# Reordering the attention head stage of a two-layer cross-attention kernel: third four's scores ahead of a projection, second four's sums ahead of the third scores by keys, one copy moved to ScalarE

## The chip, the cores and the metric

The kernel runs on one core of one Trainium2 chip. The metric is the device time in microseconds (us) of one execution. Of the kernel before there are three runs, 228.4, 233.35 and 229.08 us; their median is 229.08 us. One more execution was profiled; every duration and time of day below comes from it. Engines are named as the profile names them: PE (TensorE), PEld (its weight loads), DVE (VectorE), ACT (ScalarE), POOL (GpSimd), SP (the queue that issues most loads).

## The reference, cut to what matters

Inputs are `x` and `ctx`, both 32 x 256 x 256 in float32. Layer 0 (L0) is an attention of 16 heads of 16 columns, of which only the result for batch 0 is used: it is added to every batch. Layer 1 (L1) normalises both sides, attends over 256 keys, goes through a hidden layer of 4, and attends once more on itself.

```python
def _L0_xattn_ref(tgt, memory, Wq, Wk, Wv):
    ...
    scores = jnp.einsum('bhqd,bhkd->bhqk', q, k) * scale
    probs = jax.nn.softmax(scores, axis=-1)
    att = jnp.einsum('bhqk,bhkd->bhqd', probs, v)
    ...
    tgt2 = att[0]
    return tgt + tgt2
x = _L0_xattn_ref(x, ctx_1024, ...)
x = _L1_xattn_ref(ctx_1024, x, ...)
```

So nothing of L1 that depends on `x` can begin before L0's `att` for batch 0 is there. What depends on `ctx` alone (its normalised rows) can be made during L0.

## The kernel before, in words

The order of the work is written out by hand: the program's calls are recorded in the order of the source, each engine has its own queue and takes its instructions in that order, and waits between engines are put in where data or buffers need them.

L0 (lines 670 to 736) works on batch 0. The 16 heads go in four groups of four, `j` = 0 to 3, called fours here. For each four:

- `head_queries(j)` (L477): eight matmuls give the scores by queries, `sq`, four banks of PSUM with two halves each (L445).
- `head_maxima(j, sq, heads)` (L484): one DVE reduction per head, the negated row maximum, into `m_all` (L486). Its second argument allows a part of the heads.
- `head_less(j)` (L490): PE turns the maxima (`pm`, L493); the function it returns has DVE add them to the queries, `qmT` (L498).
- `head_keys(j)` (L500): eight matmuls give the scores by keys, `sk`, with the maxima already taken off; ACT takes the exponential of each head into `eT_h` (L507).
- `head_values(j, copy)` (L512): eight matmuls give the weighted sums and the denominators, `ph` (L357); `copy` brings them to SBUF as `col_h` (L368). The copy is ACT's unless `by_vector` (DVE) is given.
- `head_turned(j)` (L522): PE turns the sums (`pt_h`, L375); the function it returns has DVE divide (a reciprocal `rd_h`, L527, and a product into `att`, L528).

The banks for `sq` and `sk` are taken in turn from six (`four_banks`, L456), so a new group of scores waits for the maxima or exponentials of an older one. `pm`, `ph`, `pt_h`, the projection of the values (`project_values`, L427, matmul L430, copied by ACT into `v1`, L437) and the small bias product (`setup_bias`, L576: matmuls `p_b1f` L579, then the DVE sum `fc1b_all` L582) share two banks under the tag "tp".

Between these stand the preparations for L1. `stats(n)` (DVE, L211) takes the statistics of batch `n` of `ctx`, two instructions for each batch. `moments_c(q)` (POOL, L222 to L236) makes from four such batches the factors `rs_c` and `nmr_c`; it needs the statistics of all four. `even_normed` (POOL, L316) normalises even rows and `odd_normed` (ACT, L322) odd rows with these factors. `moments_ahead(2)` (L269) does part of this on DVE and has POOL compute a power (`rs_c`, L227).

L0 ends with the products for fours 2 and 3 into `att`. Then `add_attention` has POOL issue a DMA that adds `att` to four batches of `x` (L751), and `add_first` (L827) has DVE add `att` to batch 0 itself (L828) and take its statistics, after which POOL computes its `rs_x` (L227). These are followed by the steps of L1: normalised rows, scores, softmax, sums, and then the second half of L1.

Of the kernel before, what the change touches and what calls it, by code (L numbers as in the profile page):

```python
# [22 lines left out]
QB = 4  # L23
# [4 lines left out]
def tile_xattn_seq(  # L28
# [51 lines left out]
    def bank(tag, name):  # L80
        return ps.tile([P, NC, D], F32, tag=tag, name=name)
# [131 lines left out]
    def moments(st, n, name, eng=None):  # L213

        eng = eng or nc.gpsimd

        def t(what, c=1, bufs=2):
            return small.tile([P, n, c], F32, tag=f"{what}{n}", name=f"{what}_{name}", bufs=bufs)

        sm, df, sq, v4, ve, nm = t("sm", 2), t("df"), t("sq"), t("v4"), t("ve"), t("nmean")  # L220
        rs, nmr = t("rs", 1, 3), t("nmr", 1, 3)
        eng.tensor_sub(df, st[:, :, 1:2], st[:, :, 4:5])  # L222
        eng.tensor_add(sm, st[:, :, 1:3], st[:, :, 4:6])
        eng.tensor_mul(sq, df, df)
        eng.tensor_scalar(v4, sm[:, :, 1:2], 4.0 / D, 4 * EPS, ALU.mult, ALU.add)
        eng.tensor_add(ve, v4, sq)
        nc.gpsimd.tensor_tensor(  # L227
            rs.rearrange("p n o -> p (n o)"),
            ve.rearrange("p n o -> p (n o)"),
            neg_half[:, 0:n],  # L230
            ALU.pow,
        )

        def product():
            eng.tensor_scalar(nm, sm[:, :, 0:1], -0.5, 0.0, ALU.mult, ALU.add)
            eng.tensor_mul(nmr, nm, rs)  # L236

        if eng is nc.gpsimd:
            product()
            return rs, nmr  # L240
        return rs, nmr, product
# [11 lines left out]
    def stats_c(n):  # L253
        q, b = n // QB, n % QB
        statistics(st_tile(q - 1)[:, 0, b], cq_of[q][:, b])
# [5 lines left out]
    def flat(st):  # L261
        return st.rearrange("p b t c -> p (b t) c")

    def moments_c(q):
        rn = moments(flat(st_of[q - 1][:, 0]), TQ, f"c{q}")
        for b in range(QB):
            mc_of[q * QB + b] = *rn, b * NC
# [44 lines left out]
    def even_normed(*ns):  # L312
        for n in ns:
            rs, nmr, i = mc_of[n]
            row = cq_of[n // QB][:, n % QB, 0, :]
            nc.gpsimd.tensor_scalar(row, row, rs[:, i, :], nmr[:, i, :], ALU.mult, ALU.add)  # L316

    def odd_normed(*ns):
        for n in ns:
            rs, nmr, i = mc_of[n]  # L320
            row = cq_of[n // QB][:, n % QB, 1, :]
            nc.scalar.activation(  # L322
                row, row, AF.Identity, bias=nmr[:, i + 1, :], scale=rs[:, i + 1, :]
            )
# [22 lines left out]
    def by_columns(psum, name, weights, moving, copy=nc.vector.tensor_copy, by_pairs=False):  # L347
        return copy_columns(columns(psum, name, weights, moving, by_pairs), name, copy)
# [22 lines left out]
    def tokens_first(psum, src, name):  # L371

        pt = psum(f"pt_{name}")
        for t in range(NC):
            nc.tensor.transpose(pt[:, 0, t * P : (t + 1) * P], src[:, t * P : (t + 1) * P], ident)  # L375
        return pt[:, 0, :].rearrange("p (t b c) -> p t b c", t=NC, c=SL)
# [50 lines left out]
    def project_values(t, copy):  # L427
        pp = bank("tp", f"pp_v{t}")
        for dc in range(NC):
            nc.tensor.matmul(  # L430
                pp[:, t, :],
                c0T[:, dc, t * P : (t + 1) * P],
                wvT[:, dc, :],
                start=(dc == 0),
                stop=(dc == NC - 1),
            )
        copy(v1[:, t, :, 0:DK], pp[:, t, :].rearrange("p (h e) -> p h e", e=DK))  # L437

    def pair_products(*pairs):

        for t in range(NC):
            for p, lhs, rhs, dst in pairs:
                for i in range(2):
                    r = SL * (p % 2 * 2 + i)
                    nc.tensor.matmul(  # L445
                        dst[i][:, t, :],
                        lhs[r : r + SL, t * P : (t + 1) * P],
                        rhs[r : r + SL, :],
                        start=True,
                        stop=True,  # L450
                    )
# [4 lines left out]
    def four_banks(name):  # L456

        at = head_banks[0]
        head_banks[0] = (at + QB) % 6
        return [  # L460
            ps0.tile([P, NC, D], F32, tag=f"h{i}", name=f"{name}_{i}")
            if i < QB
            else bank("et", f"{name}_{i}")
            for i in ((at + n) % 6 for n in range(QB))
        ]
# [8 lines left out]
    def head_of(j, i):  # L474
        return 8 * (j // 2) + 2 * i + j % 2

    def head_queries(j):  # L477

        sq = four_banks(f"sq{j}")
        qk = qT[:, j, :], kT[:, j, :]  # L480
        pair_products((0, *qk, sq[0:2]), (1, *qk, sq[2:4]))
        return sq

    def head_maxima(j, sq, heads):  # L484
        for i in heads:
            nc.vector.tensor_reduce(  # L486
                m_all[:, j % 2, :, i, ones_at[j % 2]], sq[i], AX.X, ALU.max, negate=True
            )

    def head_less(j):  # L490
        pm = bank("tp", f"pm_{j}")
        for t in range(NC):
            nc.tensor.transpose(  # L493
                pm[:, 0, t * P : (t + 1) * P],
                m_all[:, j % 2, t].rearrange("p b c -> p (b c)"),
                ident,
            )
        return lambda: nc.vector.tensor_add(qmT[:, j % 2, :], pm[:, 0, :], qT[:, j, :])  # L498

    def head_keys(j):  # L500

        sk = four_banks(f"sk{j}")
        kq = kT[:, j, :], qmT[:, j % 2, :]
        pair_products((0, *kq, sk[0:2]), (1, *kq, sk[2:4]))
        eT_of[j] = wk.tile([P, QB, NC, D], F32, tag="eTq", name=f"eT_h{j}", bufs=2)
        for i in range(QB):
            nc.scalar.activation(eT_of[j][:, i], sk[i], AF.Exp)  # L507
# [4 lines left out]
    def head_values(j, copy=nc.scalar.copy, by_pairs=False):  # L512
        col_of[j] = by_columns(
            tp_bank,
            f"h{j}",
            lambda kt, i: v1[:, kt, head_of(j, i), :],
            eT_of.pop(j),
            copy,
            by_pairs,
        )  # L520

    def head_turned(j):  # L522
        pa = tokens_first(tp_bank, col_of.pop(j), f"h{j}")

        def weighted():
            rd = small.tile([P, NC, QB, 1], F32, tag="rdh", name=f"rd_h{j}")
            nc.vector.reciprocal(rd, pa[:, :, :, DK : DK + 1])  # L527
            nc.vector.tensor_mul(  # L528
                att.rearrange("p t (k i e d) -> p t k i e d", i=QB, e=2, d=DK)[
                    :, :, j // 2, :, j % 2, :  # L530
                ],
                pa[:, :, :, 0:DK],
                rd.to_broadcast([P, NC, QB, DK]),
            )

        return weighted
# [39 lines left out]
    def setup_bias():  # L576
        pb = bank("tp", "p_b1f")
        for dc in range(NC):
            nc.tensor.matmul(  # L579
                pb[:, 0, 0:FH], ones, b1f[:, dc, :], start=(dc == 0), stop=(dc == NC - 1)  # L580
            )
        nc.vector.tensor_add(fc1b_all, pb[:, 0, 0:FH], fc1b_bc)  # L582
# [80 lines left out]
    by_vector = nc.vector.tensor_copy  # L663

    def stats(*ns):
        for n in ns:
            stats_c(n)
# [6 lines left out]
    sq = head_queries(0)  # L674
# [5 lines left out]
    sq = head_queries(1)  # L680
    less = head_less(0)
# [8 lines left out]
    head_less(1)()  # L690
    setup_outer()
    stats(3)
    project_values(1, on_scalar)
    moments_c(0)
    even_normed(0, 1, 2, 3)
    sq = head_queries(2)
    stats(4)
    head_maxima(2, sq, (0, 1))
    head_values(0)
    setup_bias()  # L700
    head_maxima(2, sq, (2, 3))
    head_keys(1)
    odd_normed(0, 1)
    weighted = head_turned(0)
    stats(5)
    head_less(2)()
    weighted()
    sq = head_queries(3)
    stats(6)
    head_maxima(3, sq, range(QB))  # L710
    head_values(1)
    odd_normed(2, 3)
    head_keys(2)
    weighted = head_turned(1)
    stats(7)
    moments_c(1)
    even_normed(4, 5)
    head_less(3)()
    weighted()
    head_keys(3)  # L720
    stats(8, 9, 10)
    head_values(2, by_vector)
    stats(11)
    odd_normed(4)
    head_values(3, on_scalar, True)
# [1 line left out]
    weighted = head_turned(2), head_turned(3)  # L727
# [633 lines left out]
```

## Time and profile before

| what | from | us |
|---|---|---|
| median of three runs | times | 229.08 |
| the profiled execution's own time | times | 233.63 |
| its span | page | 231.9 |
| PE, DVE, ACT, POOL busy over the span | page, part 1 | 214.7, 169.8, 146.8, 174.8 |
| L0's last part, from `qmT` of the second four to the sum into batch 0 | chain | 17.65 to 34.89 |
| DVE busy in 34.90 to 48.60 | busy time by stretch | 12.33 of 13.70 |
| POOL busy in 48.60 to 96.00 | busy time by stretch | 43.67 of 47.40 |
| PE busy in 96.00 to 160.00 | busy time by stretch | 62.81 of 64.00 |

A line of the timeline reads: start, duration, engine, line of the source, operation, output and inputs, shapes, how many instructions were merged, and in brackets the idle time before it with the engine and line that ended it. Durations overlap a little with the next instruction's start, so steps are best taken from start to start. A line of the chain reads start, duration, engine, tile and line. The profiled execution is 4.55 us longer than the median of the runs; the granted clock of PE was 1.00 in every stretch up to 190 us and 0.83 in the stretch from 190.00 to 231.90, far behind the part that is changed.

### The profile page before, as it was taken

How to read it: one execution, taken by the hardware profiler on the slowest of the kernel's cores; microseconds unless marked ns; L12 is line 12 of the kernel's file. 1: busy time of each engine (PE TensorE's matmuls, PEld its weight loads, DVE VectorE, ACT ScalarE, POOL GpSimd, SP SyncE). 2: the span in 40 equal slices, each digit the busy share in tenths (PEclk: the TensorE clock that was granted, in tenths of full speed). 3: DMA queues.
4: the chain of work that ended last, by engine and by line, in shares of the span. 5: the costliest groups of instructions: out<-in, count | busy, mean ns of one | idle time of the engine just before them, and what ended most of it. 6: DMA issues, size and time to landing. Idle time of an engine off the chain costs nothing.

```text
span 231.9 us, 4950 instructions
## 1 busy us (share of the span) xinstructions
PE 214.7 (93%) x1797; PEld 155.8 (67%) x1797; DVE 169.8 (73%) x409; ACT 146.8 (63%) x299; POOL 174.8 (75%) x276
## 2 busy tenths in 40 slices
PE   7999898898999989999999999989989999999960
PEld 6766556576787768697897887866665666566540
DVE  1797989899988748667686686766384866588791
ACT  2544978698988285966789967456846753444410
POOL 6057598576989999999979999995189999993000
PEclk9999999999999999999999999999999995699996
DMA  6789997999959964180720000000000130444477
GB/s 212 271 310 371 394 383 148 194 256 236 207 104 335 275 117 170 34 151 2 133 51 1 3 0 0 3 4 4 4 0 3 51 133 0 181 184 181 185 281 264
DMA packets 18038, 33.81 MB, mean 146 GB/s; under 512 B 1175, under 2 KB 2142, under 8 KB 18014
## 3 DMA queue, kind: packets, MB, share of 16 engines
q1 hardware_dynamic: 12974, 24.33, 29.3%
q0 software_dynamic: 3696, 7.34, 18.1%
q10 hardware_dynamic: 1344, 1.84, 2.3%
q8 instruction: 14, 0.23, 0.4%
q14 instruction: 10, 0.08, 0.1%
HBM read 17.73 MB, written 8.39 MB: 113 GB/s over the span
## 4 chain that ended last, share of the span: by engine, by line
PE 53%; POOL 23%; DVE 14%; ACT 5%; issue 2%; DVEq 0%; POOLq 0%; ACTq 0%
PE sc L779 13%; POOL x_all L770 5%; PE k L445 4%; PE pt_x L202 4%; PE o L445 3%; PE pt_c L202 3%; POOL cq L307 3%; DVE st L211 3%; PE pt_e L202 3%; PE pu L357 3%; POOL rs_b L227 3%; PE sc L445 2%; POOL rs_x L227 2%; PE ph L357 2%; PE pf L357 2%
## 5 line engine op out<-in xcount | busy, mean ns | idle before, releaser
L779 PE MATMUL sc<-nxT,nfT 128*128 128x256 f32 x256 | 62.4, 386 | 0.7 <-ACT nfT L761 0.7
L779 PEld LDWEIGHTS sc<-nxT,nfT 128*128 128x128 f32 x256 | 45.7, 190 | 12.1 <-issue 5.3
L770 POOL TENSOR_TENSOR x_all<-x_all,w_bc 128x512 f32<-128x512 f32 x32 | 39.8, 1273 | 0.0
L792 ACT ACTIVATE e<-sc,nm 128x256 f32<-128x256 f32 x64 | 26.9, 473 | 19.0 <-DVE nm L789 18.8
L789 DVE TENSOR_REDUCE nm<-sc 128x2 f32<-128x512 f32 x32 | 22.0, 688 | 22.9 <-PE sc L779 11.1
L761 ACT ACTIVATE nfT<-pt_x,bq,wq 128x256 f32<-128x256 f32 x64 | 33.3, 583 | 1.6 <-PE pt_x L202 1.5
L1214 DVE TENSOR_TENSOR x_all<-o,x_all 128x512 f32<-128x512 f32 (+1 forms) x22 | 19.4, 927 | 8.0 <-PE o L445 8.0
L211 DVE BATCH_NORM_STATS2 st<-x_all 128x6 f32<-128x256 f32 x64 | 23.2, 411 | 0.6 <-DMA x_all<-att 0.5
L1209 ACT ACTIVATE eT<-k 128x1024 f32<-128x1024 f32 (+1 forms) x16 | 14.2, 916 | 13.2 <-PE k L445 10.5
L202 PE MATMUL pt_x<-ident,x_all 128*128 128x128 f32 x132 | 20.8, 280 | 1.5 <-POOL x_all L329 1.3
L202 PE MATMUL pt_c<-ident,cq 128*128 128x128 f32 x132 | 19.7, 276 | 1.5 <-ACT nfT L761 1.0
L202 PE MATMUL pt_e<-ident,e 128*128 128x128 f32 x128 | 19.5, 275 | 1.3 <-ACT eTq L801 0.7
L211 DVE BATCH_NORM_STATS2 st<-cq 128x6 f32<-128x256 f32 x56 | 20.6, 412 | 0.0
L307 POOL TENSOR_SCALAR cq<-cq,rs_b,nmr_b 128x256 f32<-128x256 f32 x32 | 19.4, 680 | 0.0
L202 PEld LDWEIGHTS pt_e<-ident,e 128*128 128x128 f32 x128 | 15.4, 141 | 5.0 <-ACT e L792 1.6
L202 PEld LDWEIGHTS pt_x<-ident,x_all 128*128 128x128 f32 x132 | 15.5, 143 | 4.7 <-POOL x_all L329 2.4
L801 ACT COPY eTq<-pt_e 128x512 f32<-128x512 f32 x32 | 18.4, 588 | 0.3 <-PE pt_e L202 0.3
L345 DVE COPY nxT<-pt_c 128x512 f32<-128x512 f32 x23 | 15.6, 677 | 2.3 <-PE pt_c L202 2.3
L202 PEld LDWEIGHTS pt_c<-ident,cq 128*128 128x128 f32 x132 | 15.0, 141 | 3.1 <-ACT nfT L761 1.9
L331 ACT ACTIVATE x_all<-x_all,nmr_b,rs_b 128x256 f32<-128x256 f32 x16 | 9.8, 618 | 10.9 <-POOL nmr_b L236 10.9
L445 PE MATMUL o<-w_out,vt 32*128 32x256 f32 x128 | 15.0, 448 | 0.6 <-ACT vt L1088 0.5
L445 PE MATMUL k<-tt,ut 32*128 32x256 f32 x112 | 15.3, 441 | 0.1
(222 smaller groups left out, 443.8 us busy)
## 6 DMA issues: line engine op xcount, KB each, us to landing
out_dram<-x_all SPq DMA_DIRECT2D x16, 512.0 KB
x_all<-att POOLq DMA_DIRECT2D x7, 1024.0 KB, 9.3
cq<-in_ctx_dram SPq DMA_DIRECT2D x6, 1024.0 KB
x_all<-in_x_dram SPq DMA_DIRECT2D x4, 1024.0 KB
x_all<-in_x_dram SPq DMA_DIRECT2D x1, 2048.0 KB
x_all<-in_x_dram SPq DMA_DIRECT2D x1, 1792.0 KB
cq<-in_ctx_dram ACTq DMA_DIRECT2D x1, 1024.0 KB
cq<-in_ctx_dram SPq DMA_DIRECT2D x1, 768.0 KB
```

The lines of the kernel that those rows point to most:

```text
L202: nc.tensor.transpose(pt[:, dc, t * P : (t + 1) * P], src[:, t, dc * P : (dc + 1) * P], ident)
L211: nc.vector.bn_stats(st[:, t, :], src[:, t, :])
L307: nc.gpsimd.tensor_scalar(row, row, rs[:, i + t, :], nmr[:, i + t, :], ALU.mult, ALU.add)
L357: nc.tensor.matmul(pg[SL * b : SL * (b + 1), 0, :], weights(kc, b), moving[:, b, kc, :], start=(kc == 0), stop=(kc == NC - 1),)
L445: nc.tensor.matmul(dst[i][:, t, :], lhs[r : r + SL, t * P : (t + 1) * P], rhs[r : r + SL, :], start=True, stop=True,)
L761: nc.scalar.activation(nfT_of[n][:, dc, :], px[:, dc, :], AF.Identity, bias=bq[:, dc : dc + 1], scale=wq2[:, dc : dc + 1],)
L770: nc.gpsimd.tensor_mul(x_all[:, n], x_all[:, n], w2_bc.unsqueeze(1).to_broadcast([P, NC, D]))
L779: nc.tensor.matmul(sc[:, qt, :], nfT[:, dc, qt * P : (qt + 1) * P], nxT[:, dc, :], start=(dc == 0), stop=(dc == NC - 1),)
L789: nc.vector.tensor_reduce(nm, sc, AX.X, ALU.max, negate=True)
L792: nc.scalar.activation(e[:, qt, :], sc[:, qt, :], AF.Exp, bias=nm[:, qt : qt + 1])
L801: nc.scalar.copy(eT_of[q][:, b], turned(e_of.pop(n), "et", f"e_{n}"))
L1214: nc.vector.tensor_add(xs, po, xs)
```

## The change

Only the list of calls of L0 is rewritten; no function changes. In the new order:

- `head_queries(2)` stands ahead of `project_values(1)`, and `setup_bias()` directly behind that projection.
- The maxima of the third four are no longer cut in two by `setup_bias()`: its four reductions stand together on DVE, behind `fc1b_all`.
- The statistics of batches 4 and 5 stand behind the third four's `qmT`, those of 6 and 7 behind the fourth four's `qmT` (before: 4 ahead of the third four's maxima, 5 behind them, 6 ahead of the fourth four's maxima, 7 behind them).
- `head_values(0)` stands behind `head_keys(1)` and behind the turned maxima of the third four; `head_values(1)` stays ahead of `head_keys(2)`.
- `head_turned(0)` stands behind the scores of the fourth four, its division behind that four's `qmT`; `head_turned(1)` stands behind the turned maxima of the fourth four, ahead of `head_keys(3)`.
- The copy of the third four's sums is ACT's instead of DVE's.

No instruction is added or removed, apart from that copy, which changes its engine; the order on POOL and SP stays as it was, and from `moments_ahead(2)` on all engines have the order they had.

```diff
     stats(3)
+    sq = head_queries(2)
     project_values(1, on_scalar)
+    setup_bias()
     moments_c(0)
     even_normed(0, 1, 2, 3)
-    sq = head_queries(2)
+    head_maxima(2, sq, (0, 1))
+    head_keys(1)
+    head_maxima(2, sq, (2, 3))
+    less = head_less(2)
+    head_values(0)
+    odd_normed(0, 1)
+    less()
     stats(4)
-    head_maxima(2, sq, (0, 1))
-    head_values(0)
-    setup_bias()
-    head_maxima(2, sq, (2, 3))
-    head_keys(1)
-    odd_normed(0, 1)
+    sq = head_queries(3)
+    stats(5)
+    head_maxima(3, sq, range(QB))
     weighted = head_turned(0)
-    stats(5)
-    head_less(2)()
-    weighted()
-    sq = head_queries(3)
-    stats(6)
-    head_maxima(3, sq, range(QB))
     head_values(1)
     odd_normed(2, 3)
     head_keys(2)
+    head_less(3)()
+    weighted()
+    stats(6)
     weighted = head_turned(1)
     stats(7)
     moments_c(1)
     even_normed(4, 5)
-    head_less(3)()
+    head_keys(3)
     weighted()
-    head_keys(3)
     stats(8, 9, 10)
-    head_values(2, by_vector)
+    head_values(2)
     stats(11)
     odd_normed(4)
     head_values(3, on_scalar, True)
```

## The prediction

> **What bounds the kernel now.** I read the page first, then the chain of work that ended last, then the timelines of the engines from 18 to 38 us, where the change lies. The chain of that stretch:
>
> ```profile
> 17.65 0.43 DVE qmT L498
> ...
> 19.26 1.08 PE sq L445 x16
> ...
> 28.51 0.44 DVE qmT L498
> ...
> 30.14 3.25 PE ph L357 x32
> 33.38 0.38 PE pt_h L375 x2
> ...
> 34.89 0.70 DVE x_all L828
> ```
>
> It runs through PE and DVE to the sum of `att` into batch 0 (L828) at 34.89. The date of that sum is what the change can move. DVE's timeline:
>
> ```profile
> 20.35 1.29 DVE L486 TENSOR_REDUCE m_all<-sq 128x2 f32<-128x512 f32 x2 [0.97 <-PE sq L445]
> 21.91 0.16 DVE L582 TENSOR_TENSOR fc1b_all<-p_b1f,fc1b_bc 128x4 f32<-128x4 f32 x1 [0.27 <-PE p_b1f L579]
> ...
> 33.79 0.21 DVE L527 RECIPROCAL rd_h<-pt_h 128x8 f32<-128x8 f32 x1 [0.61 <-PE pt_h L375]
> ```
>
> DVE works through nearly without a stop and stands idle three times only: 0.97 us for the third four's scores, 0.27 us for the bias product, 0.61 us at the end for the turned sums. POOL's and ACT's timelines:
>
> ```profile
> 28.57 0.21 POOL L222 TENSOR_TENSOR df_c<-st 128x8 f32<-128x8 f32 x1 [2.66 <-DVE st L211]
> ...
> 31.70 0.20 POOL L236 TENSOR_TENSOR nmr_c<-nmean_c,rs_c 128x8 f32<-128x8 f32 x1
> ...
> 35.17 1.51 POOL L751 DMA_DIRECT2D x_all<-att  x1 [0.28 <-DVE att L528]
> ```
> ```profile
> 32.14 0.62 ACT L322 ACTIVATE cq<-cq,nmr_c,rs_c 128x256 f32<-128x256 f32 x1
> ...
> 33.42 0.37 ACT L368 COPY col_h<-ph 128x256 f32<-128x256 f32 x1 [0.66 <-PE ph L357]
> ```
>
> POOL begins `moments_c(1)` 0.08 us after the statistics of batch 7 (end 28.49). Its last product is ready at 31.90, just before ACT wants it at 32.14 for `odd_normed(4)`; and behind that on ACT stands the copy of the fourth four's sums. Behind L0 there is no reserve: in 34.90 to 48.60 DVE is busy 12.33 of 13.70 us. POOL then waits for DVE alone:
>
> ```profile
> POOL x_all L329 <- DVE nmr_x L236: 2.4, 4, 0.9
> POOL rs_x L227 <- DVE ve_x L226: 2.1, 2, 1.2
> ```
>
> These are all of POOL's waits from 45 to 96 us, the last at 57; then it runs full, and PE from 96 to 160 (62.81 of 64.00). A delay of L828 should reach the end whole.
>
> **What the Trainium skill says.** "PSUM — Partial Sum Buffer", section "Engine vs sequencer instructions": the queues of ScalarE, VectorE and GpSimd are strict FIFO, and matmuls keep program order. The trace agrees: the second pair of maxima starts at 21.99, behind `fc1b_all`, though the second pair of scores was written in the same group as the first, reduced from 20.35. "VectorE: DVE Perf Modes", section on the perf-mode tier table: `tensor_reduce` has only the 1x form; one head's 512 values take 682 ns here, and two at 1.20 from start to start cost what four at 2.39 do, so "uncut" saves nothing in itself. "Perfetto Trace Analysis", section "Optimizing Scalar/DVE Operations": an access to PSUM costs about 125 ns more on DVE and 51 on ScalarE; the copy of sums is 406 ns on DVE and 372 on ACT, the same direction. Its section "GPSIMD Instruction" advises start-to-start times for GpSimd, which I use.
>
> **The change, step by step.** Nothing but one copy is added or removed, no DMA is moved in a queue; so everything is in the waits. I walk the new order, with steps from start to start in the trace of before.
>
> *Third four's maxima.* PE is free at 17.95 (18.13 less 0.18 of waiting). `sq` of the third four 1.08 (19.19 to 20.27), so to 19.03; the projection 1.06 (18.13 to 19.19), to 20.09; `fc1b_all` follows the start of `p_b1f` by 0.64 (21.27 to 21.91): 20.73. All four maxima now stand behind it on DVE: start 0.08 later at 20.81, four at 0.60, last end 23.29. Before it was 23.27. The scores are ready 1.24 us earlier (17.95 instead of 19.19), and the wait for the bias product takes it all: DVE, done with batch 3 at 18.73, idles about 2.0 us instead of 0.97 + 0.27. The statistics of batches 4 and 5, which filled this place or followed it, are now still undone.
>
> *Scores by keys of the second four.* Their third and fourth matmul wait for the first two maxima, whose ends are 21.49 and 22.09, so the group ends near 22.9 as before; ACT's exponentials keep their 22.97.
>
> *Turn to the fourth four.* `pm` 0.15 after the maxima (23.27 to 23.42 before): 23.44; `qmT` 0.47 to 0.50 later: 23.93, before 23.92. On PE the sums of the first four now follow `pm` (0.34 later, 23.78) and take 1.00, so the fourth four's `sq` starts at 24.78, before 23.76. Its first maximum can start 1.16 after that (19.19 to 20.35): 25.94; DVE has done batches 4 and 5 by 25.6. Before: 25.36. Four maxima end at 28.42, `pm` 28.57, `qmT` 29.04, before 28.51: **+0.53**.
>
> *PE behind it.* `pt_h` of the second four now waits for `qmT` (it takes `pm`'s bank) and stands ahead of the fourth four's scores by keys: 29.04 + 0.42 + 0.1 + 0.27 puts these at 29.85, before 28.99. Exponentials start 1.22 later: 31.07. The sums of both last fours end 3.17 after that (30.21 to 33.38 before): 34.24. ACT's added copy takes 0.27 there (33.42 to 33.69) and runs at 33.0, hidden behind the wait that follows; without it, it would cost that.
>
> *DVE behind it.* Division of the first four: 0.78 after `qmT` (28.51 to 29.29), 29.82. Statistics of batches 6 and 7, four at 0.33: the last ends at 31.22, **before 28.49, 2.7 us earlier**. Second division 0.44, batches 8 to 11 eight at 0.33 to 34.30, moments 0.86: 35.16. Then two divisions at 0.53 and 0.57 (33.79 to 34.32 to 34.89): L828 at **36.3, +1.4**, if nothing else is later.
>
> *POOL and ACT.* The statistics of batch 7 at 31.22 let POOL begin at 31.30; 3.33 (28.57 to 31.90) to its product: 34.63. `odd_normed(4)` on ACT, ready since 33.3, waits for it and takes 0.50. Only then the copy of the fourth four's sums: 35.16, though the sums are there at 34.24. Its turn 0.42 later, the reciprocal 0.48, the product 0.24, L828 0.33 (33.42, 33.84, 34.32, 34.56, 34.89): **36.63, +1.74**. This is the later path, so it decides.
>
> *What else is queued.* Behind the late moments POOL has `even_normed(4, 5)` 1.2, the power 1.64, then the first `add_attention`: 37.5 instead of 35.17. Next it serves `rs_x` for batch 0, due at 37.13 + 1.74 = 38.87; the issue takes 0.85 (37.81 to 38.66), so it is done at 38.4, hidden by 0.5. The added `x` is wanted by DVE's statistics at 48.41 + 1.74 = 50.15, 12.6 us after the issue; the page has 9.3 us to landing. Hidden too.
>
> The sum is +1.74 us on the profiled execution, whose own time is 233.63 (span 231.9): 235.37. That execution is 4.55 us longer than the median of the runs, and its granted clock fell below 1.00 (to 0.83) only behind 190 us, so I take the stretch of the change to be the same in both and add the same to 229.08: **230.8 us**, +0.8%.
>
> **Rivals.** *Other work covers POOL's delay:* were the moments ready before 33.7, DVE's own path would decide: +1.4, 230.5. For it: DVE is the fuller engine. Against: the statistics of batch 7 end 2.7 us later, and POOL had 0.24 to spare. *Later waits absorb it:* the steps of L1 in 35 to 57 us have gaps (POOL idles up to 1.2 for DVE), and if one of them ends on something not shifted, a load, up to the whole is swallowed: 229.1 to 230. Against: the chain there names no load. *Faster, the other side:* if the bias product came back before 19.2, at the third four's maxima, these would start at 19.19 (17.95 + 1.16, with DVE free), 1.6 us earlier; PE's sums and the same chain behind them take back 1.0 at `qmT` and the statistics put off another 1.3 to 1.7; at best L828 at about 34.4, -0.5: 228.6. It decides only if `p_b1f` isn't behind both `sq` and the projection on PE; it is, so that I give it little. *Over 2% slower:* the first attention transfer, 2.3 us later, lands behind 50.15, if it takes over 12.6 us among the other loads (up to 394 GB/s in the page's slices till 35 us); at 16 us it adds 3.4 to the chain: 234.2, and more with the ones behind it.
>
> **How the numbers follow.** POOL and ACT path 0.52, DVE path 0.18, absorbed 0.13, faster 0.10, late transfer 0.07. The likeliest gives 230.8, its own range 229.9 to 231.8, from 1.74 give or take a third and 0.3 of scatter (228.4 to 229.08 among the runs). For 8 in 10 it reaches down into the absorbed and the faster case and not to the late transfer: 228.2 to 232.8. Within 2% (229.08 give or take 4.6, about what a measurement of this kernel can tell from no change) lie the first three and most of the fourth: 0.92. Faster by over 2%: 0.03, for a gain behind L0 that I don't see. Slower: 0.05, most of the late transfer.
>
> **What would show it.** Right: `fc1b_all` near 20.7 with DVE idle about 2 us ahead of it; `qmT` of the fourth four at 29.0; POOL's moments at 31.3; ACT idle about 1 us ahead of `odd_normed(4)`; L828 near 36.6; the sum kept to 57 and 96 us. Wrong: maxima starting at 19.2; no idle time ahead of `odd_normed(4)`; L828 before 35; or L828 late and the end not.

## The result, and the profile after

The changed kernel takes 231.28 us in the median of six runs (230.63 to 233.13), the kernel before beside it 229.10 us (six runs). The ratio is 1.0118, with a 95% interval of 1.0074 to 1.0163: 2.2 us slower in the medians, 1.7 to 3.7 us by the interval, and by the bound of 2% the same. A few executions, such as one of 233.35 us among the six of the kernel before, belong to a slow state and are left out of the ratios. The profiled execution took 231.22 us, with a span of 229.4 us. In one of the six runs (233.13 us) PE's mean granted clock was 0.980 instead of 0.988 to 0.993; what lies behind that comes with the experiments.

Of the orders in the title one is no change: the second four's sums stood ahead of the third four's scores by keys before, too. What moved there are the first four's sums.

The whole head stage starts earlier or later from run to run: the second four's `qmT` begins between 17.14 and 18.13 us in the traces of this study. So everything below is counted from the start of the second four's `qmT` (17.65 us before, 17.77 us after). On that count the sum into batch 0 moved from 17.24 to 19.15 us, by **+1.91**.

First the timeline of DVE in the kernel after (start, duration, engine, line, operation, tiles, and in brackets the idle time before it and what ended it):

```profile
21.08 0.16 DVE L582 TENSOR_TENSOR fc1b_all<-p_b1f,fc1b_bc 128x4 f32<-128x4 f32 x1 [2.23 <-PE p_b1f L579]
21.16 2.48 DVE L486 TENSOR_REDUCE m_all<-sq 128x2 f32<-128x512 f32 x4
24.22 0.43 DVE L498 TENSOR_TENSOR qmT<-pm,qT 128x256 f32<-128x256 f32 x1 [0.59 <-ACT eT_h L507]
...
26.22 2.48 DVE L486 TENSOR_REDUCE m_all<-sq 128x2 f32<-128x512 f32 x4 [0.26 <-PE sq L445]
29.36 0.42 DVE L498 TENSOR_TENSOR qmT<-pm,qT 128x256 f32<-128x256 f32 x1 [0.65 <-ACT cq L322]
...
36.36 0.21 DVE L527 RECIPROCAL rd_h<-pt_h 128x8 f32<-128x8 f32 x1 [0.30 <-PE pt_h L375]
...
36.92 0.69 DVE L829 TENSOR_TENSOR x_all<-x_all,att 128x512 f32<-128x512 f32 x1
...
38.91 0.16 DVE L226 TENSOR_TENSOR ve_x<-v_x,sq_x 128x2 f32<-128x2 f32 x1
```

The brackets tell nearly all of it. Before, DVE stood idle 0.97 + 0.27 + 0.61 = 1.85 us between the second four's `qmT` and L828; now it is 2.23 + 0.59 + 0.26 + 0.65 + 0.30 = 4.03 us. That is 2.18 more; the copy that went to ACT gives back 0.32 (its step from start to start, below in e5_stats_late), which leaves +1.86 of the measured +1.91. DVE does no more work than before, it waits more, and over half of its waiting is one wait: the bias product.

POOL's timeline of the kernel after:

```profile
31.61 0.21 POOL L222 TENSOR_TENSOR df_c<-st 128x8 f32<-128x8 f32 x1 [5.60 <-DVE st L211]
...
34.74 0.20 POOL L236 TENSOR_TENSOR nmr_c<-nmean_c,rs_c 128x8 f32<-128x8 f32 x1
...
37.71 1.46 POOL L752 DMA_DIRECT2D x_all<-att  x1
39.16 0.77 POOL L227 TENSOR_TENSOR rs_x<-ve_x,neg_half 128x2 f32<-128x2 f32 x1
```

And ACT's:

```profile
34.97 0.60 ACT L322 ACTIVATE cq<-cq,nmr_c,rs_c 128x256 f32<-128x256 f32 x1 [1.22 <-POOL nmr_c L236]
35.48 0.35 ACT L368 COPY col_h<-ph 128x256 f32<-128x256 f32 x1
```

POOL's moments wait 5.60 us (2.66 before) for the statistics of batch 7; ACT stands idle for 1.22 us until POOL's product is there, with the last copy of sums behind it. In front of `rs_x` there is no bracket any more, and the chain of waits that ended last, below, takes the issue of the transfer for what came ahead of it. But the issue held nothing up. `rs_x` begins 0.09 us after the end of `ve_x` (39.07); before it was 0.10 us (37.03 to 37.13), with POOL idle in front of it:

```profile
36.87 0.16 DVE L226 TENSOR_TENSOR ve_x<-v_x,sq_x 128x2 f32<-128x2 f32 x1
37.13 0.72 POOL L227 TENSOR_TENSOR rs_x<-ve_x,neg_half 128x2 f32<-128x2 f32 x1 [0.45 <-DVE ve_x L226]
```

In both kernels `rs_x` follows the sum by 2.24 us. The chain after:

```profile
30.22 1.32 DVE st L211 x4
31.54 0.07 issue
31.61 0.21 POOL df_c L222
...
32.81 1.65 POOL rs_c L227
...
36.12 1.63 POOL rs_c L227
37.76 1.41 POOL x_all L752
39.17 0.77 POOL rs_x L227
39.96 0.17 DVE nmr_x L236
```

Before, the chain went through PE's sums and the division; now it goes through the late statistics and POOL's moments. From there it reaches `rs_x` over DVE's part of `moments_ahead(2)`, POOL's power and the transfer's issue; the other path, over ACT's copy and the sum to `ve_x`, ends at the same place within 0.1 us. Behind that, POOL's two largest waits from 45 to 97 us are those of before, to the tenth:

```profile
POOL x_all L329 <- DVE nmr_x L236: 2.4, 4, 0.9
...
POOL rs_x L227 <- DVE ve_x L226: 2.1, 2, 1.2
```

POOL's third normalised row (L329) starts at 50.69 us instead of 48.59, PE's step at 96.05 at 98.08; counted from the `qmT` that is 1.98 and 1.91 us later. Nothing is absorbed on the way to the end.

### The profile page after: what moved, and what is told of

The parts are those of the page before. It is cut to its first block, busy times and chain, and to the rows that moved or that the text cites. A ratio compares the mean times of both kernels' runs of the same rounds, so it can differ in the third digit from the quotient of the medians.

```text
span 229.4 us, 4953 instructions
## 1 busy us (share of the span) xinstructions
PE 211.2 (92%) x1797; PEld 153.9 (67%) x1797; DVE 169.5 (74%) x408; ACT 147.0 (64%) x300; POOL 174.5 (76%) x276
## 4 chain that ended last, share of the span: by engine, by line
PE 54%; POOL 17%; DVE 10%; ACT 4%; issue 2%; DVEq 0%; POOLq 0%; ACTq 0%
PE sc L780 15%; PE k L445 5%; PE o L445 4%; PE pu L357 4%; PE pt_e L202 3%; POOL cq L307 3%; PE pt_x L202 3%; PE pt_c L202 3%; PE q L445 3%; DVE st L211 3%; PE pv L357 3%; POOL rs_b L227 3%; PE sc L445 2%; POOL rs_c L227 2%; POOL rs_x L227 2%
## 5 line engine op out<-in xcount | busy, mean ns | idle before, releaser
L445 PE MATMUL o<-w_out,vt 32*128 32x256 f32 x128 | 14.0, 401 | 0.6 <-ACT vt L1089 0.5
L445 PE MATMUL k<-tt,ut 32*128 32x256 f32 x112 | 13.1, 399 | 0.1
```

Source lines behind the costliest of these rows:

```text
L445: nc.tensor.matmul(dst[i][:, t, :], lhs[r : r + SL, t * P : (t + 1) * P], rhs[r : r + SL, :], start=True, stop=True,)
```

## The experiments

One table first, since all runs are read on the same scale. "Moments" is the start of POOL's `df_c`, "sum" is L828 (L829 or a line beside it), "first row" is POOL's first L329, all in us from the second four's `qmT`; "idle" is DVE's idle time between that and the sum. The ratio is to the kernel before on the same chip.

| kernel | moments | sum | rs_x | first row | idle | ratio (95%) |
|---|---|---|---|---|---|---|
| before | 10.92 | 17.24 | 19.48 | 24.62 | 1.85 | 1 |
| after | 13.84 | 19.15 | 21.39 | 26.61 | 4.03 | 1.0118 (1.0074 to 1.0163) |
| e2_bias_later | 12.88 | 18.18 | 20.41 | 25.63 | 3.06 | 1.0031 (1.0009 to 1.0054) |
| e3_stats_early | 12.33 | 18.95 | 21.19 | 26.33 | 3.59 | 1.0102 (1.0060 to 1.0144) |
| e8_bias_odd_later | 12.88 | 17.82 | 20.25 | 26.18 | 2.77 | 1.0068 (1.0045 to 1.0092) |
| e4_copy_only | 10.92 | 17.23 | 19.47 | 24.62 | 1.89 | 0.9998 (0.9981 to 1.0016) |
| e5_stats_late | 12.69 | 18.00 | 20.24 | 25.47 | 2.59 | 1.0043 (1.0026 to 1.0060) |
| e7_all | 10.16 | 17.25 | 19.49 | 24.63 | 2.03 | 1.0032 (1.0008 to 1.0056) |
| e9_keys_first | 10.15 | 16.73 | 18.97 | 24.17 | 1.43 | 0.9994 (0.9976 to 1.0012) |

**e0_before**, the kernel before with no edit, for the scale.

> The kernel before, unchanged, profiled once more, to set its trace beside the changed kernel's. Theory (the 2.0 us lost in the head stage ride the chain to the end and nothing else changes): the sum of att into batch 0 starts at 34.9 to 35.1; the chain leaves POOL at 93.2 to 93.5; with the granted clock near 1.00 behind 190 us its time is 228.4 to 229.5, about 2.0 under the changed kernel's 231.2. Rival (a second loss further back): with equal clocks the gap between the two grows behind 96 us to 2.7 or more.

It took 229.76 us at a span of 228.0; its sum stands at 17.24, its first row at 24.63 and its idle time is 1.85 us again. The trace repeats to 0.01 us once the start is taken off. From the `qmT` to the end of the span it is 209.9 us here and 211.6 us in the kernel after, at mean clocks of 0.987 and 0.990: +1.7, so that no second loss further back shows.

**e2_bias_later**: the bias product behind the third four's turned maxima.

```diff
     project_values(1, on_scalar)
-    setup_bias()
     moments_c(0)
...
     less()
+    setup_bias()
     stats(4)
```

> The changed kernel with setup_bias() put behind the third four's turned maxima and the first four's sums; the third four's maxima no longer stand behind the bias product. Theory (that wait of 2.2 us takes the gain of the earlier scores): DVE idles 0.7 us instead of 2.2 ahead of these maxima, which start at 19.6 to 19.9 instead of 21.16; qmT of the fourth four comes 1.0 us earlier, at 28.3, and with it POOL's moments (30.6), the sum into batch 0 (35.9) and the end; the time falls by 1.0. Rival (PE is the limit, so the maxima start earlier but the fourth four's scores don't): qmT of the fourth four stays at 29.2 to 29.4 and the time doesn't change.

Measured: 229.94 us (11 runs), sum -0.97. DVE's timeline:

```profile
18.69 2.48 DVE L486 TENSOR_REDUCE m_all<-sq 128x2 f32<-128x512 f32 x4 [0.41 <-PE sq L445]
...
23.31 0.16 DVE L582 TENSOR_TENSOR fc1b_all<-p_b1f,fc1b_bc 128x4 f32<-128x4 f32 x1 [1.06 <-PE p_b1f L579]
```

The maxima now start 1.49 us after the `qmT`, 3.39 in the changed kernel. Of these 1.9 us half is lost again on the way to the sum, partly to the 1.06 us that DVE waits for the same product at its new place. So the wait for the bias product makes about half of the whole loss.

**e3_stats_early**: in the changed kernel, the statistics of batches 6 and 7 back ahead of the fourth four's `qmT`.

```diff
     head_keys(2)
+    stats(6, 7)
     head_less(3)()
     weighted()
-    stats(6)
     weighted = head_turned(1)
-    stats(7)
```

> The changed kernel with the statistics of batches 6 and 7 back ahead of the fourth four's qmT. Theory (they cost where they stand because POOL and ACT wait for them, but DVE has 0.65 us of idle time ahead of qmT only): qmT moves from 29.36 to 30.0, POOL's moments start at 30.0 instead of 31.6, ACT no longer waits for them, the sum into batch 0 starts at 36.6 and the time falls by 0.3. Rival (the late statistics are the whole loss): the sum starts near 35.3 and the time falls by 1.5 or more.

Measured: 231.0 us (6 runs), sum -0.20. The moments come 1.51 us earlier and ACT's wait is gone, as its timeline shows:

```profile
33.68 0.41 ACT L368 COPY col_h<-ph 128x256 f32<-128x256 f32 x1
33.93 0.64 ACT L322 ACTIVATE cq<-cq,nmr_c,rs_c 128x256 f32<-128x256 f32 x1
35.01 0.37 ACT L368 COPY col_h<-ph 128x256 f32<-128x256 f32 x1 [0.44 <-PE ph L357]
```

But the fourth four's `qmT` is 0.58 us later, and now ACT waits for PE's sums. Two paths of nearly the same length end here, and shortening one at the cost of the other gained 0.20 us.

**e5_stats_late**: the same question from the other side, in the kernel before.

```diff
     sq = head_queries(3)
-    stats(6)
     head_maxima(3, sq, range(QB))
...
-    stats(7)
-    moments_c(1)
-    even_normed(4, 5)
     head_less(3)()
     weighted()
+    stats(6, 7)
+    moments_c(1)
+    even_normed(4, 5)
```

> The kernel before with one thing alone: the statistics of batches 6 and 7 are put behind the fourth four's qmT and the first division, as the changed kernel has them. Theory (POOL's moments wait for them and odd_normed(4) on ACT for POOL): the fourth four's qmT comes about 0.46 to 0.6 us earlier; POOL's moments start about 1.7 us later than in the kernel before (30.2 against 28.57 on its clock); ACT stands idle ahead of odd_normed(4); L828 about 0.7 us later (17.9 from the second four's qmT); time +0.75 us. Rival (DVE's own work alone sets L828, so that a changed order of the same work costs nothing): L828 within 0.2 of 17.24, the time within 0.3 us of the kernel before.

Measured: 230.24 us (15 runs), sum +0.76, the fourth four's `qmT` 0.43 us earlier. POOL's timeline of this kernel:

```profile
29.93 0.21 POOL L222 TENSOR_TENSOR df_c<-st 128x8 f32<-128x8 f32 x1 [4.43 <-DVE st L211]
```

ACT's:

```profile
33.29 0.60 ACT L322 ACTIVATE cq<-cq,nmr_c,rs_c 128x256 f32<-128x256 f32 x1 [1.85 <-POOL nmr_c L236]
33.80 0.35 ACT L368 COPY col_h<-ph 128x256 f32<-128x256 f32 x1
```

And DVE's, where the copy's step to the next instruction is 0.32 us:

```profile
31.73 0.41 DVE L368 COPY col_h<-ph 128x256 f32<-128x256 f32 x1
32.05 0.74 DVE L211 BATCH_NORM_STATS2 st<-cq 128x6 f32<-128x256 f32 x2
```

DVE's work is only reordered, its `qmT` is even earlier, and still the sum is late: the wait runs from DVE's statistics over POOL's moments to ACT, and ACT's copy stands behind it. The path that the prediction let decide is shown here alone.

**e4_copy_only**: the kernel before, with the third four's sums copied by ACT.

```diff
-    head_values(2, by_vector)
+    head_values(2)
```

> The kernel before with one part of the change alone: both halves of the third four's sums are copied by ScalarE. Counted from the second four's qmT, L828 stood at 17.24 us in the kernel before. Theory (the copy is hidden on both engines): DVE's idle time ahead of the reciprocal of the third four's sums grows from 0.61 by up to the 0.4 us of the copy taken away, ACT stays ahead of the fourth four's sums, L828 stays within 0.15 of 17.24, the time within 0.3 us of the kernel before. Rival (the second copy on ACT delays odd_normed(4) and so the fourth four's copy): L828 +0.3, time +0.3.

Measured: 229.25 us (12 runs), sum at 17.23, DVE's idle time at the end 0.65 instead of 0.61. The copy alone costs and gains nothing; DVE got only 0.04 us of idle time out of it at that place; small instructions ahead of it took longer, such as `sm_c` with 0.38 us instead of 0.17.

**e1_odd_later**: in the changed kernel, ACT's `odd_normed(4)` behind the copy of the fourth four's sums, so that the copy no longer waits for POOL.

```diff
-    odd_normed(4)
     head_values(3, on_scalar, True)
+    odd_normed(4)
```

> The changed kernel with odd_normed(4) put behind the copy of the fourth four's sums, so that this copy no longer stands behind ACT's wait for POOL's moments. Theory of the prediction (that wait sets the end of L0, 0.3 us behind DVE's own path): the sum into batch 0 starts 0.3 us earlier, at 36.6, and the time falls by 0.3. Rival, from the changed kernel's chain (POOL's own queue, power 1.6 and DMA issue 1.4 behind the late moments, ends at 39.16 and holds the factors of batch 0): the sum starts at 36.6 but rs_x stays at 39.1 and the time falls by 0.1 at most. Second rival (DVE alone decides): the sum stays at 36.9.

Measured: 233.57 us (4 runs), ratio 1.0203 (1.0172 to 1.0234), so *slower* by 2.3 us. But the trace shows something else, more than 10 us ahead of the edit. Busy time and granted clock by stretches (columns: stretch, wall share, busy share and count of PE, PEld, DVE, ACT, POOL, then PE's granted clock, DMA share, GB/s):

```profile
21.00:22.00 1.00, 0.69 (x8) 0.37 (x6) 1.00 (x3) 0.00 (x0) 1.00 (x1) 1.00 1.08 387
22.00:23.00 1.00, 1.00 (x10) 0.91 (x10) 1.00 (x2) 0.00 (x0) 0.92 (x3) 0.56 1.02 322
23.00:24.00 1.00, 1.00 (x6) 0.35 (x3) 0.00 (x1) 0.89 (x2) 0.89 (x3) 0.50 1.04 387
...
28.00:29.00 1.00, 1.00 (x10) 0.39 (x10) 0.63 (x2) 0.00 (x0) 0.00 (x0) 0.53 1.05 385
29.00:30.00 1.00, 1.00 (x20) 0.42 (x20) 1.00 (x3) 0.00 (x0) 0.00 (x0) 1.00 1.05 385
```

PE's granted clock falls to 0.50 for 6.8 us, and the sum stands at 21.57. Up to 34 us every engine has the order of the changed kernel, so that no step of the edit comes ahead of the fall; the run suggests that the changed kernel can do this.

**a0_after**: the changed kernel once more.

> The changed kernel once more, unchanged, for how often PE's granted clock falls in it. Theory (the idle time on PE that the wait for the bias product brings lets the clock fall to 0.50 for some 6 us in some runs): of its runs some, a fifth to a half, stand near 233 at a mean clock of 0.974 to 0.981, the others near 231 at 0.985 to 0.993. Rival (the four runs of e1_odd_later and two of e3_stats_early were of that kernel or of the hour): no run stands at a mean clock of 0.974 to 0.984.

Measured: 231.49 us (6 runs), ratio 1.0109 (1.0062 to 1.0157); two of the six at 233.3 and 233.4 us with a mean clock of 0.975 and 0.976. The profiled execution was taken at 0.976, and its stretches show the same fall:

```profile
21.00:22.00 1.00, 0.69 (x4) 0.30 (x3) 1.00 (x3) 0.00 (x0) 0.99 (x1) 1.00 0.98 301
22.00:23.00 1.00, 1.00 (x10) 0.91 (x10) 1.00 (x2) 0.00 (x0) 0.92 (x3) 0.61 1.05 383
23.00:24.00 1.00, 1.00 (x7) 0.35 (x3) 0.07 (x1) 0.88 (x2) 0.89 (x3) 0.50 1.04 391
...
28.00:29.00 1.00, 1.00 (x10) 0.36 (x10) 0.61 (x1) 0.00 (x0) 0.00 (x0) 0.50 1.05 387
```

So it belongs to the changed kernel, in some of its executions; here the sum stands at 21.94, 2.79 us behind the execution without it.

This also gives e1 its proper partner, since both have the fall: with `odd_normed(4)` later the sum is at 21.57 instead of 21.94, **-0.37**, but POOL's first row at 29.92 instead of 29.39, **+0.53**.

**e8_bias_odd_later**: the edits of e1 and e2 together.

> The edits of e1_odd_later and e2_bias_later together: the changed kernel with the bias product behind the third four's turned maxima, and odd_normed(4) behind the fourth four's copy. On the clock: theory (the fall of PE's granted clock to 0.50 from 22 to 28 us that e1 showed comes of PE's idle time behind the wait of the scores by keys for maxima that stand behind the bias product): no slice under 0.9 before 160 us in any run. Rival (it comes of the edit behind 34 us, or of chance): the clock falls here too. On the waits: e2 had L828 at 18.18 us from the second four's qmT, with ACT idle 1.21 us ahead of odd_normed(4). If ACT's wait decides L828, it comes at 17.4 to 17.8, and DVE's own work is next; if POOL's own queue (moments, power, attention issue) decides what follows, then rs_x is no earlier than in e2 (20.41 from the second four's qmT) and the time is within 0.3 us of e2's 229.9 whatever L828 does.

Measured: 230.74 us (5 runs), no fall of the clock (in the profiled execution no slice under 0.9 ahead of 160 us; mean clocks of the five 0.984 to 0.991). Against e2 the sum is at 17.82 instead of 18.18, **-0.36**, `rs_x` at 20.25 instead of 20.41, and the first row at 26.18 instead of 25.63, **+0.55**: the pair of numbers that e1 gave against a0, without the fall. ACT's wait cost 0.36 us at the sum, as the first theory had it. Of that 0.16 us were left at `rs_x`, but not because POOL's queue decided, as the rival had it: `rs_x` begins 0.09 us after the end of `ve_x`, as in the other traces. It is DVE's `v_x` that took 0.36 us here, 0.16 in e2. That the end is 0.8 us *later* than e2's neither had said: the time is 230.74 us against 229.94. DVE's timeline of e8:

```profile
36.97 0.36 DVE L225 TENSOR_SCALAR v_x<-sm_x 128x2 f32<-128x2 f32 x1
37.37 0.16 DVE L226 TENSOR_TENSOR ve_x<-v_x,sq_x 128x2 f32<-128x2 f32 x1
...
38.61 0.34 DVE L236 TENSOR_TENSOR nmr_x<-nmean_x,rs_x 128x2 f32<-128x2 f32 x1 [0.41 <-POOL rs_x L227]
38.99 1.01 DVE L329 TENSOR_SCALAR x_all<-x_all,rs_x,nmr_x 128x256 f32<-128x256 f32 x1
```

And POOL's:

```profile
36.36 1.46 POOL L752 DMA_DIRECT2D x_all<-att  x1
37.62 0.96 POOL L227 TENSOR_TENSOR rs_x<-ve_x,neg_half 128x2 f32<-128x2 f32 x1
...
39.15 2.37 POOL L316 TENSOR_SCALAR cq<-cq,rs_c,nmr_c 128x256 f32<-128x256 f32 x2
```

DVE's row takes 1.01 us where e2 and the kernel after have 0.69 and 0.68, POOL's two rows 2.37 where they have 1.67; they lie on each other for 0.85 us, in e2 for 0.16. From the sum to POOL's first row it is 8.36 us, in e2 7.45. Four steps, from start to start, make 0.89 of these 0.91 us: `v_x` 0.20, `rs_x` 0.19, `nmr_x` 0.18 and DVE's row 0.32. The Trainium skill, "GPSIMD Engine Reference", section "1. Specifications", says that GpSimd's interfaces to SBUF are shared with VectorE and that some of VectorE's instructions contend with it there. The stretched durations fit that; which of the instructions it was, no run took apart. Lying on each other is not enough by itself: in e2 `v_x` starts during the transfer's issue, too (37.16, the issue from 36.16), and takes 0.16 us.

**e6_sums_behind**: in the changed kernel, the fourth four's scores by queries ahead of the first four's sums on PE.

```diff
-    head_values(0)
-    odd_normed(0, 1)
     less()
     stats(4)
     sq = head_queries(3)
+    head_values(0)
+    odd_normed(0, 1)
```

> The changed kernel with one thing undone: the fourth four's scores by queries ahead of the first four's sums on PE. The prediction put 0.53 us of qmT on this order. Theory (with the statistics of batches 4 and 5 still undone, DVE can't take the fourth four's maxima much earlier than the sums allow): fourth four's scores 1.0 us earlier on PE, its maxima only 0.3 us earlier (as soon as the statistics of batch 5 are done), its qmT at 11.2 to 11.5 us from the second four's (11.59 changed, 10.86 before), L829 0.1 to 0.3 us earlier than the 19.15 of the changed kernel, time -0.1 to -0.3 us. Rival (PE's order holds the maxima): qmT a whole 0.5 us or more earlier, L829 and the time -0.5.

Measured: 232.39 us (4 runs, 231.26 to 237.76), ratio 1.0117 (1.0069 to 1.0165). The clock fell in the profiled execution, from 24.2 to 27.6 us, so its steps can't be compared with the changed kernel's undisturbed ones, nor with those of a0, where the fall lasts twice as long. The two runs at mean clocks of 0.987 and 0.993 took 231.48 and 231.26 us, where the changed kernel has 230.6 to 231.3 in all but one of such runs of its first series: neither the 0.1 to 0.3 us of the theory nor the 0.5 of the rival is seen. What the order of these two groups is worth by itself stays open.

**e10_fill**: the changed kernel with two idle matmuls more behind the bias product, to fill the time in which PE waits for maxima.

```diff
         nc.vector.tensor_add(fc1b_all, pb[:, 0, 0:FH], fc1b_bc)
+        pd = bank("tp", "p_fill")
+        nc.tensor.matmul(pd[:, 0, :], ident, qT[:, 0, :], start=True, stop=True)
+        nc.tensor.matmul(pd[:, 1, 0:P], ident, qT[:, 0, 0:P], start=True, stop=True)
```

> The changed kernel with two matmuls more (256 and 128 columns, the identity by q, into a bank that nothing reads) behind the bias product, where PE otherwise runs out of work until the third four's maxima are there; nothing else is changed, and no output depends on them. They should take about 0.8 us of the time in which PE waits anyway. Theory (the thin stretch on PE, a bias product of four columns and the wait behind it, lets the granted clock fall to 0.50 for some 5 us): of all runs so far with the bias product ahead of the third four's maxima 11 or 12 of 26 stood at a mean clock of 0.963 to 0.981, of 30 with it later none; with the fill no run stands there, and all come at 230.6 to 231.5. Rival (the fall has another cause, such as the load before it, or comes by chance): about two in five runs still show it, at 232.3 to 233.4. In both the waits are as they were: bias product 3.3 us after the second four's qmT, L829 (L832 here) at 19.1 to 19.3 in a run without the fall.

Measured: 231.21 us (6 runs, 230.29 to 232.1), ratio 1.0103 (1.0072 to 1.0134); mean clocks 0.987 to 0.990 in all six, the sum at 19.22. PE's timeline of this kernel:

```profile
20.08 0.51 PE L579 MATMUL p_b1f<-b1f,ones 128*128 128x4 f32 x4
20.84 0.70 PE L584 MATMUL p_fill<-qT,ident 128*128 128x256 f32 x2 [0.25 <-DVE fc1b_all L582]
21.38 0.39 PE L585 MATMUL p_fill<-qT,ident 128*128 128x128 f32 x2
21.69 1.53 PE L445 MATMUL sk<-qmT,kT 32*128 32x256 f32 x16
```

The fill waited for `fc1b_all` and left a gap of 0.25 us ahead of itself, so it thickened the stretch but did not close it. In the runs with the bias product ahead of the third four's maxima and no fill, the mean clock was 0.963 to 0.981 in 11 of 26 (after 1 of 6, a0 2 of 6, e1 4 of 4, e3 2 of 6, e6 2 of 4); in e2, e8 and e9, with the product later, in none of 30. Three of the eleven were profiled and show the fall; for the others it is inferred from the mean. With the fill it was none of 6, which at 11 in 26 happens by chance in 4 of 100 such series, (15/26)^6. But four of the eleven are e1's, and at the changed kernel's own 3 in 12 it happens in 18 of 100, (9/12)^6. And e7 below has the product later still, and eight of its 22 runs are some 2 us longer at a mean clock of 0.984 to 0.985, with no trace of one. So the thin stretch as the cause of the fall is a suspicion, not shown.

**e7_all** and **e9_keys_first**: can the early scores be made to pay? e7 puts the bias product behind the third four's sums, the statistics of batch 4 ahead of the third four's maxima, those of batch 6 ahead of the fourth four's `qmT`, the second four's sums and divisions later, and `odd_normed(4)` behind the last copy.

```diff
     sq = head_queries(2)
     project_values(1, on_scalar)
-    setup_bias()
...
+    stats(4)
     head_maxima(2, sq, (0, 1))
...
     head_values(2)
+    setup_bias()
```

> The changed kernel's early scores without what they were held by: third four's scores ahead of the projection, the bias product only behind the third four's sums, the second four's scores by keys and turned maxima ahead of the first four's later work, statistics spread so that batch 4 fills the time ahead of the third four's maxima and 6 comes ahead of the fourth four's qmT, odd_normed(4) behind the fourth four's copy. Theory (the early scores are worth something where no wait stands behind them): third four's maxima start 1.0 to 1.6 us after the second four's qmT (3.39 in the changed kernel), L828 at 16.0 to 16.6 us from it (17.24 before, 19.15 changed), time 0.6 to 1.2 us below the kernel before. Rival (DVE is full in this stretch, so that no order is worth more than its idle 1.85 us, and new waits take that): L828 within 0.3 of 17.24, the time within 0.4 of the kernel before.

Measured: 230.31 us (22 runs), and at the sum the rival held: the fourth four's `qmT` stands 1.87 us earlier than in the kernel before (8.99 against 10.86), the sum where it was (17.25). PE's timeline shows where it went:

```profile
30.82 0.61 PE L579 MATMUL p_b1f<-b1f,ones 128*128 128x4 f32 x4
32.46 1.09 PE L357 MATMUL ph<-eT_h,v 128*32 128x256 f32 x16 [1.03 <-ACT col_h L368]
```

The last sums waited 1.03 us for a copy on ACT that stood behind `odd_normed(3)` and the exponentials. Eleven of its runs stood at 228.5 to 229.6 us, eight at 231.1 to 231.2 at a mean clock of 0.984 to 0.985, and three at 233.5 to 233.7; the trace is of one of the eleven. e9 orders the tail anew:

```diff
     weighted = head_turned(0)
-    head_values(1)
+    odd_normed(2)
+    head_keys(3)
     stats(7)
...
+    head_values(1, by_vector)
+    setup_bias()
...
     head_values(3, on_scalar, True)
+    odd_normed(3)
     odd_normed(4)
```

> The kernel e7_all, whose fourth four's qmT stood 1.87 us earlier than in the kernel before while L830 stood where it was, with the tail reordered: the fourth four's scores by keys right behind its qmT and ahead of the second four's sums, these copied by VectorE, odd_normed(2) ahead of the last exponentials and odd_normed(3) behind the last copy on ACT. Theory (e7's gain was lost because the copies of sums on ACT stood behind odd_normed and the exponentials, and the last sums waited 1.03 us for the copy of the third four's): last sums end at 14.0 to 14.5 us from the second four's qmT (15.6 in e7), L830 at 15.7 to 16.3 (17.25 in e7, 17.24 before), time 0.8 to 1.4 us below the kernel before. Rival (DVE's own work sets L830): within 0.3 of 17.24 again, and the time within 0.4 of the kernel before.

Measured: 228.96 us (14 runs; before 229.43), ratio 0.9994 (0.9976 to 1.0012); sum at 16.73, first row at 24.17, 0.45 us ahead of the kernel before. Of the 0.9 to 1.5 us that the theory expected at the sum, 0.51 came. At the end a gain of 0.45 us, 0.2%, would lie inside the interval, which can't tell it from none. It beats the changed kernel, and the kernel before not measurably. `rs_x` follows the sum by 2.24 us, as in the kernels before and after.

## Why the prediction was right

It said 230.8 us and +1.74; measured are 231.28 us, +2.2 in the medians, and, in the trace, +1.91 at the sum and +1.99 at POOL's first row. Sign, place and size were right. By its own steps, with its dates counted from 17.65:

- *The wait for the bias product takes all of the early scores.* Right: DVE idle 2.23 us (predicted about 2.0), and e2 shows what it costs. `fc1b_all` came at 3.31, predicted 3.08. The term that was mis-sized is `sq` of the third four, for which 1.08 us from a free PE were put in. It took 1.76. Its later banks are those of the first four's scores by keys, and 0.20 us stand in the profile as a wait for that four's exponentials; where the rest of the 0.68 us more went the profile does not show (PE's weight loads in the kernel after):

```profile
18.51 0.72 PEld L445 LDWEIGHTS sq<-kT,qT 32*128 32x128 f32 x10 [0.20 <-ACT eT_h L507]
```

 PE came free 0.26 us earlier than put in, and the next two steps were 0.19 shorter, so that of the missing 0.68 us only +0.23 was left. That these two made good most of it was luck. The +0.23 runs through the rest: the fourth four's scores came 0.16 us later than predicted, its `qmT` 0.20, POOL's moments 0.19, the last copy on ACT 0.20 and the sum 0.17.
- *The fourth four's `qmT` +0.53.* Measured +0.73 (11.59 against 10.86), with that stall in it. That PE's order of sums and scores makes it was argued; e6 couldn't test it.
- *Statistics of batch 7 late, POOL's moments late, ACT behind them, as the later of two paths.* Right in each link: moments 13.84 (13.65 predicted), ACT idle 1.22 us ("about 1"). That DVE's own path was 0.33 us shorter (36.3 against 36.63) is what e1 and e8 measured when they took ACT's wait away, 0.37 and 0.36. e5 shows the path alone.
- *The copy by ACT costs nothing.* Right (e4).
- *The transfer's issue is hidden by 0.5 us.* Hidden it was: `rs_x` waited for `ve_x` and not for the issue (0.09 us after its end, before 0.10). The size of the reserve isn't known. The 0.85 us from start to start were those of the second transfer. In e8 and e1 `rs_x` begins 1.26 us after the start of the first, again just behind `ve_x`, so that the issue holds POOL for at most that; here `rs_x` begins 1.45 us after it (37.71 to 39.16), which leaves a reserve of at least 0.19 us.
- *Nothing absorbed behind.* Right: from the `qmT` 1.99 at the first row, 1.98 at POOL's L329 of 48.59, 1.91 at PE's step of 96.05. The late transfer to 234 us did not come about: no wait for a DMA stands among the larger ones from 45 to 97 us.
- *Not foreseen:* the fall of PE's clock that comes in some executions of the changed kernel and costs 2 to 3 us more. It is no part of the +1.74, which undisturbed executions show.

What stays open: why the clock falls, whether for the bias product's thin matmuls, the gap behind them or something else; and why DVE and POOL take 0.9 us longer from the sum to the first row when the sum comes 0.36 us earlier.

## What to carry to other kernels

Moving a result forward is worth what stands *behind* it in the consumer's queue: four maxima that could start 1.2 us earlier than before (e2) gained nothing, because one small sum that needed a product from far back in PE's queue stood ahead of them on DVE. When cheap filler (here statistics) is moved behind the critical work, look up who reads it on the other engines; the 2.9 us of delay at POOL's moments came back over POOL and ACT as a wait in front of the last copy. And measure a stage by one event at its far end, counted from one at its near end: here that resolved 0.01 us, where the times of whole runs scatter over 1 us.

## What was unexpected in the hardware

PE's granted clock fell from 1.00 to 0.50, for 6.8 us in the traces of e1 and a0 and for 3.4 us in that of e6, in the middle of a stage in which PE had been busy in every stretch since 17 us but for some 0.31 us in one. The Trainium skill, "TensorE: Matmul & The Clock Gate", section "HAM oscillation — how this bites in real kernels", gives gaps of more than some 3.4 us as what lets the clock drop; its section "A second HAM failure mode: psum-queue depth-cycling" tells of a kernel in which short idle times between groups were enough. The 0.50 agrees with its half rate. The first rule does not fit these traces; the second may, though only one such gap stands between 17 us and the fall, and the kernel after has the same gap of 0.32 us in its trace without a fall. It was not steady: by the trace or the mean clock the same kernel showed it in 3 of 12 executions, and e1, the same up to 34 us, in 4 of 4; at 3 in 12 four of four would be a chance of 0.4 in 100, and why e1 showed it each time stays open.

Small DVE instructions doubled in time: `v_x`, 128x2, took 0.36 us in e8 and 0.37 in e1, and 0.16 in e2 and the kernel after. And the duration that the profile shows for the issue of a transfer by POOL is not the time for which it holds POOL's queue: the first transfer of e8 is shown with 1.46 us, and the next instruction began after 1.26; the second of the kernel after with 1.39, and the next began after 0.85 (39.84 to 40.69).
